# Turning the rows of a second norm by transfers and one VectorE transpose, with the chains around it started three steps sooner

## The chip, the cores and the metric

The kernel runs on one core of a Trainium2 chip. The metric is the device time of one execution in microseconds. Kernels are compared by the median of several executions; the profile is that of one further execution.

## What is computed

Four blocks follow each other on x, which has 8 batch rows of 128 tokens with 512 features. Each block adds a gated update to x, and each reads a layer norm of x:

```
x = x + tanh(g_xattn[0]) * xattn0(layernorm(x), ctx, mask, ...)   # 32 heads of 128
x = x + tanh(g_ffn[0])   * ffn0(layernorm(x), ...)                # 4-bit weights, 512 -> 512
x = x + tanh(g_xattn[1]) * xattn1(layernorm(x), ctx, ...)         # one head of 512
x = x + tanh(g_ffn[1])   * ffn1(layernorm(x), ...)                # dense + routed low-rank update

def xattn1(text, features):
    fn = rmsnorm(features, fn_w)
    Q = rmsnorm(text @ Wq.T + Wq_b, qn_w)
    K = rmsnorm(fn @ Wk.T + Wk_b, kn_w)
    return softmax(Q @ K.T / sqrt(512)) @ fn

def layernorm(x):
    return (x - mean(x)) / sqrt(var(x) + 1e-5)
```

All of it is float32. The kernel gets that accuracy from TensorE by splitting every operand into a high part (type fp32r) and a low part, and by three matmuls for a product: high by high, high by low, low by high.

## The kernel before

The first attention with its weights takes about 765 of the 904 us. What follows is written as chains, one Python generator for a batch row and a block: `ffn0(b)` (L1238), `keys(b)` (L1210, the keys of the second attention), `xattn1(b)` (L1248) and `ffn1(b)` (L1299). `pipeline` (L48) advances all running chains by one step in turn, the newest first. The list `starts` (L1470) says in which step a chain begins. `ffn0(b)` begins in step b + 1 and makes its product psf two steps on; `xattn1(b)` begins in step b + 9; `ffn1(b)` in step b + 17. The weights of `ffn1` are loaded by `ffn1_weights` (L1403), begun in step 13.

TensorE follows the order in which this code issues its instructions (`in_order`, L147). The other engines and the queues follow a planner, which takes what is ready first in a simulated run and, among the ready ones, what the code issued first. `behind(name)` (L140) orders an instruction behind the last one that was marked with that name on the same engine. `mark("x", ...)` stands in `add_to_x` (L793), the VectorE instruction L797 that adds a block's product to x.

The norm is `layernorm` (L1159). In its first step ScalarE writes the row minus its mean to a tile t of 128 tokens by 512 features (L1170). In the second, TensorE turns the four 128 by 128 blocks of t into PSUM (`transposed`, L1143, tile name tph in the trace), ScalarE casts them to the high part and VectorE subtracts for the low part (`parts_of`, L1153, through `split`, L168), tile name h1T, h2T or h3T. Then ScalarE squares the row for its sum (L1177), into a tile that nothing reads ("junkh", in buffers with the tag "raw"), and GpSimd turns the sum into an inverse root (`inverse_root`, L419). The third step makes the product: `dense` in `xattn1` gives psq, and VectorE scales it and adds the bias into q (L1253). In `ffn0` the product is psf; there GpSimd first adds the bias row to x (`add_row`, L1189, ordered behind the last inverse root), and L797 adds the product.

Operands of the products lie in tiles with the tag "page", of which there are 14: two for the transposed keys, two for the query weights, four for the context rows (fn), one for each hT, and four with one more for the weights of `ffn1` (bw, lora). A load into a page waits on its queue until a page comes free.

The first norm of the kernel, ahead of the first attention, turns its rows in another manner. `send` (L457) writes a tile to DRAM and reads it back with 32-row blocks exchanged: one write, and one read for each of four groups of 32 partitions, all issued from the queue of SyncE. `turned` (L470) then transposes every 32 by 32 block by one VectorE instruction (L473). `by_rows` (L449) is the layout in which the rows are written for this.

Of the kernel before, what the change touches and what calls it, by code (L numbers as in the profile page):

```python
# [13 lines left out]
AF = mybir.ActivationFunctionType  # L14
ALU = mybir.AluOpType
AX = mybir.AxisListType

P = 128
NB = 8
D = 512  # L20
NDC = D // P
# [6 lines left out]
Q32 = 32  # L28
NQ = P // Q32
# [37 lines left out]
def kernel(  # L67
# [37 lines left out]
    nc = tc.nc  # L105
# [9 lines left out]
    def slot(shape, tag, name, dtype=F32):  # L115
        return sb.tile(shape, dtype, tag=tag, name=name, bufs=TAGS[tag])
# [6 lines left out]
    def wide_row(tag, name, dtype=F32):  # L123
        return slot([P, D], tag, name, dtype)
# [4 lines left out]
    def wide(t):  # L129

        return t.bitcast(F32)
# [4 lines left out]
    def mark(name, inst):  # L136
        marks[name] = inst.ins

    @contextmanager
    def behind(*names):  # L140
        with ExitStack() as stack:
            for name in names:
                stack.enter_context(tc.issue_after(marks[name]))
            yield
# [238 lines left out]
    for inner in range(2):  # L383
        for half in range(2):
            for dc in range(inner * HK, inner * HK + HK):
                if half == 0 and dc == inner * HK:
                    load_half(0, inner)
                t = wide_row("wo", f"cxraw{half}{dc}")
                queue = nc.scalar if dc == half == 0 else nc.sync
# [5 lines left out]
    lnw = wide_row("pT", "lnw")  # L395
# [40 lines left out]
    def row_stats(j):  # L436
# [9 lines left out]
        nc.gpsimd.tensor_tensor(shift, mean, r12, ALU.mult)  # L446
        nc.gpsimd.tensor_scalar_mul(shift, shift, -1.0)

    def by_rows(t):  # L449

        return t.rearrange("p (n dc k) -> p dc n k", n=NQ, dc=NDC)
# [2 lines left out]

        return t.rearrange("p b (n k) -> p n b k", k=Q32)

    def send(b, name, t, tag):  # L457

        through = dram.tile([P, NQ, NDC * Q32], F32, tag="rows", name=f"rows_{name}_{b}", bufs=6)
        nc.sync.dma_start(out=through, in_=t.rearrange("p (n f) -> p n f", n=NQ))  # L460
        moved = slot([P, NQ, NDC, Q32], tag, f"{name}moved_{b}")
        blocks = through.rearrange("(i q) n f -> n q i f", q=Q32)
        for j in range(NQ):
            move = nc.sync.dma_start(
                out=moved[bass.ts(j, Q32)].rearrange("p i b k -> p i (b k)"), in_=blocks[j]
            )
        mark("sent", move)
        return moved

    def turned(b, name, moved, tag):  # L470

        t = slot([P, NDC, P], tag, f"{name}turned_{b}")
        nc.vector.transpose(by_block(t), moved)  # L473
        return t

    def normed(b):
        xq_b = wide_row("wo", f"xq_{b}")
        nc.scalar.activation(
            xq_b, xs[b], AF.Identity, bias=stats[:, b, 5:6], scale=stats[:, b, 2:3]
        )  # L480
        rows = wide_row("wo", f"xrows_{b}")
        nc.vector.tensor_tensor(
            by_rows(rows), *(t.rearrange("p (dc n k) -> p dc n k", n=NQ, dc=NDC) for t in (xq_b, lnw)), ALU.mult
        )
        return send(b, "x", rows, "s")

    def right_pages(name):
        return {n: page([P, 2, HK, HALF * P], f"{name}{n}") for n in RIGHT.values()}
# [482 lines left out]
    rows = []  # L971
# [171 lines left out]
    def transposed(b, name, src):  # L1143
        tag = "sc" if b % 2 and name in SC_NAMES else "av"
        tp = ptile([P, NDC, P], tag, f"tp{name}_{b}")
        for dc in range(NDC):
            nc.tensor.transpose(tp[:, dc, :], src[:, bass.ts(dc, P)], ident)  # L1147
        return tp

    def work(b, name, tag, shape=(P, D), dtype=F32):  # L1150
        return slot(list(shape), tag, f"{name}_{b}", dtype)

    def parts_of(b, name, src):  # L1153

        t = work(b, name, "page", (P, NDC, 2, P), F32R)
        split(t[:, :, 0, :], t[:, :, 1, :], src)
        return t

    def layernorm(b, name, gate=None):  # L1159


        negm = col(f"nm{name}", b)
        nc.scalar.mul(negm, col(f"sum{name}", b), -1.0 / D)
        t = work(b, name, "wo")
        src, dst = xs[b], t
        if name == "h1":

            dst = t.rearrange("p (jj a r) -> p r a jj", jj=NDC, a=2)
            src = src.rearrange("p (r a jj) -> p r a jj", a=2, jj=NDC)
        nc.scalar.activation(dst, src, AF.Identity, bias=negm)  # L1170
        yield
        tp = transposed(b, name, t)
        if name == "h3" and b > 2:
            turns.pop(b - 3)()
        hT = parts_of(b, f"{name}T", tp)
        ss = col(f"ss{name}", b)
        nc.scalar.activation(  # L1177
            work(b, f"junk{name}", "raw"), xs[b], AF.Square, bias=negm, accum_out=ss
        )
        r = col(f"r{name}", b)  # L1180
        inverse_root(r, ss, 1e-5)
        rg = r
        if gate is not None:
            rg = col(f"rg{name}", b)
            nc.gpsimd.tensor_tensor(rg, r, gate, ALU.mult)
        yield
        return hT, r, rg
# [9 lines left out]
        return ps  # L1197

    def inverse_rms(b, name, src):
        junk = work(b, f"junk{name}", "raw")  # L1200
        ss = col(f"ss{name}", b)
        mark("rms", nc.scalar.activation(junk, src, AF.Square, accum_out=ss))
        r = col(f"ir{name}", b)
        inverse_root(r, ss, 1e-6)
        return r
# [42 lines left out]
    def xattn1(b):  # L1248
        half, j = divmod(b, HALF)
        hT, rh, _ = yield from layernorm(b, "h2")  # L1250
        ps = dense(b, "q", hT, wq1_p)
        q = work(b, "q", "wo")
        nc.vector.scalar_tensor_tensor(q, ps, rh, bq, ALU.mult, ALU.add)  # L1253
        r = inverse_rms(b, "q", q)
        nc.gpsimd.tensor_scalar_mul(r, r, float(D) ** -0.5)
        yield
        tp = transposed(b, "q", q)
        qT = work(b, "qT", "v", (P, NDC, P))
        nc.scalar.copy(qT, tp)
        yield  # L1260
        sc = ptile([P, P], "sc", f"s1_{b}")
        for fc in range(NDC):
            nc.tensor.matmul(
                sc,
                lhsT=qT[:, fc, :],
                rhs=kTs[half][:, fc, j, :],
                start=(fc == 0),
                stop=(fc == NDC - 1),
            )
        p = work(b, "p1", "v", (P, P))  # L1270
        nc.scalar.copy(p, sc)
        nm = col("nm1", b)
        nc.vector.tensor_reduce(nm, p, AX.X, ALU.max, negate=True)
        nc.vector.tensor_tensor(nm, nm, r, ALU.mult)
        yield
        sm = col("sm1", b)
        nc.scalar.activation(p, p, AF.Exp, bias=nm, scale=r, accum_out=sm)
        rs = col("rs1", b)
        nc.vector.reciprocal(rs, sm)
        nc.vector.tensor_tensor(rs, rs, tgx1, ALU.mult)  # L1280
        yield
        tp = ptile([P, P], "av", f"tpp1_{b}")
        nc.tensor.transpose(tp, p, ident)
        pT = work(b, "pT1", "v", (P, 2, P), F32R)

        rc = rcs[:, b : b + 1]
        nc.scalar.activation(pT[:, 0, :], tp, AF.Copy, scale=rc)
        nc.vector.scalar_tensor_tensor(
            pT[:, 1, :], tp, rc, wide(pT[:, 0, :]), ALU.mult, ALU.subtract
        )  # L1290
        yield
        av = ptile([P, D], "mm", f"av1_{b}")
        product(av, [((pT[:, 0, :], pT[:, 1, :]), fns[b])])
        add_to_x(b, av, rs, "h3")
        yield
# [107 lines left out]
    def ffn1_weights():  # L1403
        for dc in range(NDC):
            t = page([P, 2, 2, NS], f"bw{dc}")
            nc.sync.dma_start(out=wide(t).rearrange("p a h n -> p a (h n)"), in_=bw_kept[:, dc])
            for half in range(2):
                bw[dc, half] = [t[:, part, half] for part in range(2)]
        t = page([P, 2, D], "lora")
        nc.sync.dma_start(out=wide(t), in_=lora_kept)  # L1410
        lora.extend(t[:, part] for part in range(2))
        nc.sync.dma_start(out=rb, in_=router_b.partition_broadcast(P))

        em_i = keep([P, NR], "em_i", I32)
        nc.sync.dma_start(out=em_i, in_=expert_map.partition_broadcast(P))
        em_f = keep([P, NR], "em_f")
        nc.vector.tensor_copy(em_f, em_i)
        e_i = slot([P, NE, NR], "moved", "e_i", I32)
        nc.gpsimd.iota(e_i, pattern=[[1, NE], [0, NR]], base=0, channel_multiplier=0)
        nc.vector.tensor_copy(twice, e_i)  # L1420
        nc.vector.tensor_tensor(
            twice, twice, em_f.unsqueeze(1).to_broadcast([P, NE, NR]), ALU.is_equal
        )
        nc.vector.tensor_scalar_mul(twice, twice, 2.0)
        yield
# [43 lines left out]

    starts = [[ending()], ffn[:1], ffn[1:2], ffn[2:3], [ffn[3], key[0]]]  # L1470
    starts += [[ffn[b], key[b - 3]] for b in range(4, NB)]
    starts += [[att[0], key[5]], [att[1], key[6]], [att[2], key[7]]] + [[c] for c in att[3:] + last]
    starts[6].append(query_weights())
    starts[13].append(ffn1_weights())
    with in_order(*ORD):
        pipeline(starts)

# [71 lines left out]
```

## Time and profile before

| | before |
|---|---|
| median of 3 runs | 905.67 us (905.53 to 907.04) |
| the profiled execution's own time | 906.13 us |
| its span, first to last instruction | 904.3 us |
| mean granted clock of TensorE | 0.999 |
| transposes tph, all three norms | 96, median 272 ns long |
| L1170, row minus mean, ScalarE | 24, median 725 ns |
| L170, low part of h2T, VectorE | 8, median 681 ns |
| L169, high part of h2T, ScalarE | 8, median 587 ns |
| L473, VectorE transpose of 128x512 | 8, median 706 ns |
| L1192, row addition on GpSimd | 32 of 128x256, median 740 ns |

The span is what the profile's rows cover; the execution's own time is 1.8 us longer. A row names a line of the kernel, an engine, an operation, the tiles written and read, and a duration. TensorE overlaps neighbouring matmuls, so what one costs is the distance between starts and not its length. In rows of waits, "<-" names what ended the wait.

### The profile page before, as it was taken

How to read it: one execution, taken by the hardware profiler on the slowest of the kernel's cores; microseconds unless marked ns; L12 is line 12 of the kernel's file. 1: busy time of each engine (PE TensorE's matmuls, PEld its weight loads, DVE VectorE, ACT ScalarE, POOL GpSimd, SP SyncE). 2: the span in 40 equal slices, each digit the busy share in tenths (PEclk: the TensorE clock that was granted, in tenths of full speed). 3: DMA queues.
4: the chain of work that ended last, by engine and by line, in shares of the span. 5: the costliest groups of instructions: out<-in, count | busy, mean ns of one | idle time of the engine just before them, and what ended most of it. 6: DMA issues, size and time to landing. Idle time of an engine off the chain costs nothing.

```text
span 904.3 us, 16418 instructions
## 1 busy us (share of the span) xinstructions
PE 897.8 (99%) x5349; PEld 796.7 (88%) x5349; DVE 676.9 (75%) x1361; ACT 502.0 (56%) x1422; POOL 463.1 (51%) x513
## 2 busy tenths in 40 slices
PE   9999999999999999999999999999999999999998
PEld 7887888888888899999999999999999998888897
DVE  7898887778889866777677667766686877565587
ACT  6666565666655555545536345453554544588862
POOL 2455543123323436747748567593766844265441
PEclk9999999999999999999999999999999999999999
DMA  8666568888765957577485765755756566713001
GB/s 285 220 215 224 198 217 296 276 278 302 259 229 203 310 180 209 162 213 219 154 236 154 211 209 159 214 186 184 216 176 205 174 186 181 299 47 143 1 24 71
DMA packets 130982, 179.19 MB, mean 198 GB/s; under 512 B 17744, under 2 KB 59472, under 8 KB 129872
## 3 DMA queue, kind: packets, MB, share of 16 engines
q1 hardware_dynamic: 130752, 177.88, 61.9%
q8 instruction: 42, 0.69, 0.3%
q14 instruction: 44, 0.36, 0.1%
q10 hardware_dynamic: 144, 0.26, 0.1%
HBM read 111.96 MB, written 66.13 MB: 197 GB/s over the span
## 4 chain that ended last, share of the span: by engine, by line
PE 96%; DVE 2%; ACT 1%; DMA 0%; issue 0%; DVEq 0%; ACTq 0%
PE c_v L178 7%; PE c_v L179 6%; PE c_v L182 6%; PE pso L182 6%; PE pso L178 6%; PE pso L179 6%; PE sc L712 6%; PE av L776 6%; PE c_q L178 6%; PE c_q L182 6%; PE c_q L179 6%; PE c_k L178 5%; PE c_k L179 5%; PE c_k L182 5%; PE tph L1147 1%; PE c_k L617 1%
## 5 line engine op out<-in xcount | busy, mean ns | idle before, releaser
L729 ACT ACTIVATE s<-s,nm 128x128 f32<-128x128 f32 x256 | 99.8, 392 | 79.0 <-DVE nm L719 55.8
L797 DVE SCALAR_TENSOR_TENSOR x<-pso,tg,x 128x512 f32<-128x512 f32 x128 | 93.5, 741 | 51.2 <-PE pso L182 50.4
L737 POOL TENSOR_TENSOR s<-s,rs 128x512 f32<-128x512 f32 x64 | 66.7, 1043 | 113.4 <-DVE rs L735 54.8
L178 PE MATMUL pso<-wo_h,a 128*128 128x512 f32 x256 | 101.9, 411 | 0.0
L179 PE MATMUL pso<-wo_l,a 128*128 128x512 f32 x256 | 101.5, 397 | 0.0
L182 PE MATMUL pso<-wo_h,a 128*128 128x512 f32 x256 | 101.0, 395 | 0.1
L178 PE MATMUL c_v<-wvP,cxT 128*128 128x256 f32 x288 | 84.8, 294 | 0.3 <-ACT v L253 0.3
L182 PE MATMUL c_v<-wvP,cxT 128*128 128x256 f32 x288 | 81.4, 283 | 0.0
L179 PE MATMUL c_v<-wvP,cxT 128*128 128x256 f32 x288 | 81.4, 283 | 0.0
L777 ACT CAST a<-av 128x512 fp32r<-128x512 f32 x64 | 37.3, 584 | 75.3 <-PE av L776 74.9
L699 POOL TENSOR_TENSOR s<-mneg,bias 128x512 f32<-128x512 bf16 x64 | 75.5, 1180 | 0.3 <-PE pso L182 0.3
L776 PE MATMUL av<-pT,v 128*128 128x128 f32 x512 | 71.2, 274 | 0.0
L776 PEld LDWEIGHTS av<-pT,v 128*128 128x128 f32 x512 | 67.1, 191 | 2.8
L712 PE MATMUL sc<-k,q 128*128 128x128 f32 x464 | 65.8, 274 | 0.0
L712 PEld LDWEIGHTS sc<-k,q 128*128 128x128 f32 x464 | 61.9, 191 | 3.2
L178 PE MATMUL c_v<-wvP,cxB 128*128 128x256 f32 x216 | 62.1, 289 | 0.0
L778 DVE TENSOR_TENSOR a<-av,a 128x512 fp32r<-128x512 f32 x64 | 43.4, 679 | 24.8 <-ACT a L777 24.5
L179 PE MATMUL c_v<-wvP,cxB 128*128 128x256 f32 x216 | 61.2, 283 | 0.0
L182 PE MATMUL c_v<-wvP,cxB 128*128 128x256 f32 x216 | 61.1, 283 | 0.0
L182 PEld LDWEIGHTS pso<-wo_h,a 128*128 128x128 f32 x256 | 48.2, 188 | 10.8 <-DVE a L778 1.3
L170 POOL TENSOR_TENSOR wo_l<-raw_wo,wo_h 128x512 fp32r<-128x512 f32 x32 | 41.4, 1292 | 31.2 <-ACT wo_h L169 31.2
L715 DVE TENSOR_TENSOR s<-sc,s 128x512 f32<-128x512 f32 x64 | 43.7, 683 | 17.2 <-PE sc L712 12.3
(275 smaller groups left out, 2810.5 us busy)
## 6 DMA issues: line engine op xcount, KB each, us to landing
keys<-keys SPq DMA_DIRECT2D x64, 256.0 KB, 3.3
queries<-queries SPq DMA_DIRECT2D x64, 256.0 KB, 3.1
through<-s SPq DMA_DIRECT2D x64, 256.0 KB, 2.3
moved<-through SPq DMA_DIRECT2D x256, 64.0 KB, 3.0
q<-queries SPq DMA_DIRECT2D x58, 256.0 KB, 3.9
k<-keys SPq DMA_DIRECT2D x58, 256.0 KB, 4.3
raw_wq<-in_wq_dram SPq DMA_DIRECT2D x32, 256.0 KB, 4.0
raw_wv<-in_wv_dram SPq DMA_DIRECT2D x32, 256.0 KB, 4.8
```

What stands on the lines that cost most here:

```text
L170: mark("low", (low_engine or nc.vector).tensor_tensor(low, src, wide(high), ALU.subtract))
L178: nc.tensor.matmul(out, lhsT=lh, rhs=rh, start=first, stop=False, **more)
L179: nc.tensor.matmul(out, lhsT=lh, rhs=rl, start=False, stop=False, **more)
L182: nc.tensor.matmul(out, lhsT=ll, rhs=rh, start=False, stop=last, **more),
L699: nc.gpsimd.tensor_tensor(s, mneg[:, half], bias.unsqueeze(2).to_broadcast([P, NQ, HALF, Q32]), ALU.add)
L712: nc.tensor.matmul(ps[:, j, :], lhsT=q[:, cols], rhs=k[:, cols], start=True, stop=True)
L715: nc.vector.tensor_tensor(s, by_block(ps), s, ALU.add)
L729: e = nc.scalar.activation(one, one, AF.Exp, bias=nm[:, j : j + 1], accum_out=sm[:, j : j + 1])
L737: mark(f"norm{u}", nc.gpsimd.tensor_tensor(s, s, factors, ALU.mult))
L776: nc.tensor.matmul(av[:, b, :], lhsT=v[:, cols], rhs=pT[:, b, :], start=True, stop=True)
L778: mark("al", nc.vector.tensor_tensor(al, av, wide(ah), ALU.subtract))
L797: "x", nc.vector.scalar_tensor_tensor(xs[b], ps, factor, xs[b], ALU.mult, ALU.add, **out)
```

## The change

It touches the second norm (name "h2", in `xattn1`) alone, and the order around it. The centring copy L1170 writes t in the layout of `by_rows`. In the same step t is sent through DRAM, the write issued from ScalarE's queue and the reads from SyncE's. Three steps with nothing in them are added, and `xattn1(b)` begins in step b + 6, so that the turning stays in step b + 10 as before. There one VectorE transpose takes the place of the four on TensorE; it is ordered behind the last instruction marked "x". The split then reads SBUF in place of PSUM. The moved and the turned rows take buffers with the tag "raw", and the squares of all norms write to one tile "junk" with the tag "kq". The query result L1253 is now marked "x" too. `ffn1_weights` begins in step 14, and its loads of bw and lora are ordered behind the last read of `send` ("sent"). In `starts` the chains `keys(5)` to `keys(7)` keep their steps.

```diff
+    def of_rows_by_block(t):
+        return t.rearrange("p (dc n k) -> p dc n k", n=NQ, dc=NDC)
...
-    def send(b, name, t, tag):
+    def send(b, name, t, moved, queue=nc.sync):
 
         through = dram.tile([P, NQ, NDC * Q32], F32, tag="rows", name=f"rows_{name}_{b}", bufs=6)
-        nc.sync.dma_start(out=through, in_=t.rearrange("p (n f) -> p n f", n=NQ))
-        moved = slot([P, NQ, NDC, Q32], tag, f"{name}moved_{b}")
+        queue.dma_start(out=through, in_=t.rearrange("p (n f) -> p n f", n=NQ))
...
+    def blocks_tile(tag, name):
+        return slot([P, NQ, NDC, Q32], tag, name)
...
+    junk = wide_row("kq", "junk")
...
+        far = name == "h2"
+        if far:
+            dst, src = by_rows(t), of_rows_by_block(src)
         nc.scalar.activation(dst, src, AF.Identity, bias=negm)
-        yield
-        tp = transposed(b, name, t)
+        if far:
+            moved = send(b, name, t, blocks_tile("raw", f"{name}moved_{b}"), nc.scalar)
+        yield
+        for _ in range(3 * far):
+            yield
+        if far:
+            with behind("x"):
+                tp = turned(b, name, moved, "raw")
+        else:
+            tp = transposed(b, name, t)
...
         nc.scalar.activation(
-            work(b, f"junk{name}", "raw"), xs[b], AF.Square, bias=negm, accum_out=ss
+            junk, xs[b], AF.Square, bias=negm, accum_out=ss
         )
...
     def inverse_rms(b, name, src):
-        junk = work(b, f"junk{name}", "raw")
...
-        nc.vector.scalar_tensor_tensor(q, ps, rh, bq, ALU.mult, ALU.add)
+        mark("x", nc.vector.scalar_tensor_tensor(q, ps, rh, bq, ALU.mult, ALU.add))
...
             t = page([P, 2, 2, NS], f"bw{dc}")
-            nc.sync.dma_start(out=wide(t).rearrange("p a h n -> p a (h n)"), in_=bw_kept[:, dc])
+            with behind("sent"):
+                nc.sync.dma_start(
+                    out=wide(t).rearrange("p a h n -> p a (h n)"), in_=bw_kept[:, dc]
+                )
...
         t = page([P, 2, D], "lora")
-        nc.sync.dma_start(out=wide(t), in_=lora_kept)
+        with behind("sent"):
+            nc.sync.dma_start(out=wide(t), in_=lora_kept)
...
-    starts += [[att[0], key[5]], [att[1], key[6]], [att[2], key[7]]] + [[c] for c in att[3:] + last]
+    starts += [[key[b]] for b in range(5, NB)] + [[] for _ in range(5)] + [[c] for c in last]
+    for b in range(NB):
+        starts[6 + b].insert(0, att[b])
     starts[6].append(query_weights())
-    starts[13].append(ffn1_weights())
+    starts[14].append(ffn1_weights())
```

More of the change, by code (lines that the diff above doesn't have):

```diff
@@ L481, in normed @@
         rows = wide_row("wo", f"xrows_{b}")
[L482 to L485, printed above, removed]
+        nc.vector.tensor_tensor(by_rows(rows), of_rows_by_block(xq_b), of_rows_by_block(lnw), ALU.mult)
+        return send(b, "x", rows, blocks_tile("s", f"xmoved_{b}"))
     def right_pages(name):
```

## Prediction, made before the changed kernel was run

> **What bounds the kernel now.** I read the busy shares first, then the windows from 787 us on, TensorE's waits there, and last the timelines of TensorE, GpSimd and VectorE around 814 to 821 us, where the change begins to act. Shares and one window:
>
> ```profile
> PE 897.8 (99%) x5349; PEld 796.7 (88%) x5349; DVE 676.9 (75%) x1361; ACT 502.0 (56%) x1422; POOL 463.1 (51%) x513
> ...
> 797.40:820.85 23.45, 23.45 (x126) 19.70 (x125) 16.14 (x38) 18.11 (x48) 21.28 (x45) 1.00 0.28 94
> ```
>
> TensorE sets the end. In the window (columns: length, then busy time of PE, PEld, DVE, ACT, POOL, then clock, DMA share and GB/s) it never pauses, and the one wait found for it after 760 us is 0.3 us. But POOL is at 21.28 of 23.45 us in the same stretch, a share that its 51% over the span hides. TensorE's timeline there (columns: start, length, instruction):
>
> ```profile
> 813.34 0.60 PE L1147 MATMUL tpk<-ident,k 128*128 128x128 f32 x4
> 813.78 0.60 PE L1147 MATMUL tph<-ident,h 128*128 128x128 f32 x4
> 814.14 0.48 PE L178 MATMUL psf<-wf,h1T 128*128 128x512 f32 x1
> 814.45 0.39 PE L179 MATMUL psf<-wf,h1T 128*128 128x512 f32 x1
> 814.68 0.39 PE L182 MATMUL psf<-wf,h1T 128*128 128x512 f32 x1
> ...
> 816.98 0.60 PE L1147 MATMUL tpk<-ident,k 128*128 128x128 f32 x4
> 817.42 0.60 PE L1147 MATMUL tph<-ident,h 128*128 128x128 f32 x4
> 817.77 0.48 PE L178 MATMUL psq<-wq,h2T 128*128 128x512 f32 x1
> ...
> 820.59 0.60 PE L1147 MATMUL tpk<-ident,k 128*128 128x128 f32 x4
> ```
>
> The reader should read starts, not lengths. The tph at 813.78 belongs to the second norm of batch row 0, the one at 817.42 to row 1; the psf block from 814.14 is row 7's first feed-forward product, and psq from 817.77 is row 0's query product. What stands around them on GpSimd and VectorE:
>
> ```profile
> 797.40 0.19 POOL L421 TENSOR_SCALAR cols<-cols 128x1 f32<-128x1 f32 x1 [12.53 <-ACT junkk L1202]
> ...
> 816.90 0.55 POOL L426 TENSOR_TENSOR cols<-cols,neghalf 128x1 f32<-128x1 f32 x1
> 817.42 1.44 POOL L1192 TENSOR_TENSOR x<-x,bias 128x256 f32<-128x256 f32 x2
> ...
> 817.28 0.69 DVE L170 TENSOR_TENSOR h2T<-tph,h2T 128x512 fp32r<-128x512 f32 x1
> 818.89 0.75 DVE L797 SCALAR_TENSOR_TENSOR x<-psf,cols,x 128x512 f32<-128x512 f32 x1 [0.92 <-POOL x L1192]
> ```
>
> Row 7's product is done at 816.98, but its addition to x (L797) waits for GpSimd's row addition and starts at 818.89. Row 0's low part (h2T at 817.28) stands ahead of that addition on VectorE.
>
> **What is removed.** Thirty-two TensorE transposes. Their length (272 ns) is not their price, since they overlap. A block moves the next start by 0.36 us (813.78 to 814.14), and the matmul behind it takes 0.31 us to its follower where the steady step is 0.23: together 0.44 us, the same as from tpk to tph. Eight blocks: 8 x 0.44 = 3.5 us, all on the path, in a stage where TensorE never pauses. The Trainium skill ("VectorE: DVE Perf Modes", The three transpose paths) gives 390 ns for a 128x128 bf16 transpose on TensorE; by that the 32 would be an estimated 12.5 us. The row says a quarter of it.
>
> **What is added.** *VectorE*: eight transposes of 128x512, 0.70 us each by the same operation at L473 and L761, 5.6 us; VectorE is busy 5.1 to 8.7 of every 10 us in 810 to 870, so the time itself hides there. *ScalarE*: the centring copies (0.72 us) move forward, and the eight writes to DRAM are issued from its queue, 0.40 us each by the one such issue in the trace (L390), about 0.47 with the broken overlap between two activations (0.72 long, 0.62 apart): 8 x 0.47 = 3.8 us. In 797 to 821 ScalarE waits 4.4 + 0.8 = 5.2 us, 1.05 to 1.28 us a step before L1163. One copy and one issue (0.62 + 0.47 = 1.1) just fit into such a gap. *SyncE*: 32 reads, 0.43 us to issue; between 800 and 815 us its queue issues nothing and stands before bw, which is moved, and a round trip (2.1 us write, four issues, 2.1 us landing, rows L460 and L464) takes 6 us of the four steps of 3.6 us it is given. The weights that would stand ahead of the reads (bw, lora, at 815.80 and 824.42, waiting on pages) are put behind the last read and one step later; they land in 5.3 us and are first used at 856.0, so that is hidden. If that cover failed, each microsecond late is one on TensorE. The scratch output in one buffer, written by ScalarE alone in order, and the splits that now read SBUF I cost at nothing; a cast is 0.57 us from PSUM and a square of 128x512 from SBUF 0.62, so the bounds are 0 and 0.05 x 8.
>
> **The new wait.** VectorE's transpose of row 0 is ordered behind the last addition marked "x" when it is traced. The order in that step is newest chain first, so it is row 7's feed-forward addition, the one at 818.89. Behind the transpose stand the cast, the low part and, on TensorE, whose order is fixed, psq of row 0. The addition frees VectorE at 819.57; two semaphore instructions 0.1, transpose 0.70, cast 0.57, handing on 0.2: psq starts at about 821.15, and its low part, done at about 821.7, is needed by the third matmul, 0.55 later, just so. TensorE arrives at 817.77 less two removed blocks (0.88) plus tpk, which now comes ahead (0.44): 817.33. It waits 3.8 us. This one wait costs 3.8 against 3.5 saved. Row 1 waits for the same addition but has psq of row 0 before it; rows 2 to 7 are behind the query result two rows back (L1253), with 3.7 us of TensorE work (psq 2.8, two blocks of 0.44) for 2.9 us of chain (0.75 + 0.70 + 0.57 + 0.68 and 0.2 to hand on).
>
> Two smaller terms. GpSimd runs from 797.40 to 820.85 without a wait, and what starts it is the square on ScalarE that follows row 0's centring copy; the new issue stands between them. Bounds 0 and 0.47; I take 0.4, as the copy stands directly before that square already. Key rows on VectorE (two of 0.44 us) or the next transpose (0.70) may go ahead of a low part: 0 to 0.7, I take 0.2, since 0.4 us of slack stands in most steps.
>
> **The clock.** What a pause of 3.8 us does to it no row in mid-span shows. Both ends of the span do:
>
> ```profile
> 903.00:903.50 0.50, 0.00 (x0) 0.00 (x0) 0.00 (x0) 0.00 (x0) 0.00 (x0) 0.86 0.11 33
> 903.50:904.00 0.50, 0.00 (x0) 0.00 (x0) 0.00 (x0) 0.00 (x0) 0.00 (x0) 0.50 0.00 0
> ```
>
> The last matmul ends at 900.78; the granted clock falls to 0.50 at about 903.4, 2.6 us later. At the start, nine matmuls of 128x512 from 5.28 to 9.19 step by 0.43 us instead of 0.23 (the clock column says 1.00 there all the same): 9 x 0.20 = 1.8 us. So the bounds are 0 and 1.8; a pause of 3.8 is nearer to the 2.6 that brought the fall than to the 0.3 that didn't, and I take 1.8. The Trainium skill ("TensorE: Matmul & The Clock Gate", Why this matters for your kernels) warns of pauses over about 3 us, which speaks against this change; its Part 1 has a free-running window of 3.4 us that must be idle. By that window a pause of 3.8 us would fall on a whole one about one time in ten, an estimate, and the sum would lack the 1.8.
>
> **Sum.** -3.5 + 3.8 + 0.4 + 0.2 + 1.8 = +2.7 us. The profiled execution has a span of 904.3 and a time of 906.13, 1.8 around it; it becomes a span of 907.0 and 908.8. It lies 0.46 above the median of 905.67, so the median becomes 908.4 us, slower by 0.3%.
>
> **Rivals.**
> *The clock holds.* The same wait without the fall: +0.9, 906.6. For it: the pause is not much longer than 2.6 us, and parts of it may be cut. Against: the row at the end of the span.
> *The gain stays (the other side).* Row 0's addition is not late: if GpSimd's row additions came 2 us sooner, the wait shrinks to 1.8 us or, with the transpose outside that order, to none, -3.5 to -1.7, and no clock falls. 902.2 at best, 902.7 with the small terms. For it: ScalarE loses a copy a step from 820 us on, and TensorE's work is less by a sure 3.5 us. Against: GpSimd's 21.28 of 23.45 us, and nothing taken off it. It decides from 1.7 us of wait downwards.
> *Rows that come late.* Seven "raw" buffers hold five moved rows and two turned ones, so rows 6 and 7 are read only once a turned row is split, and the bw pages queue behind these reads. Also ScalarE: 3.8 + 5 x 0.62 = 6.9 us more in 797 to 821 against 5.2 us of waits, so the GpSimd chain may slip by up to 1.7 in place of the 0.4: +4.0; with one row late by 0.5 besides, +4.5: 910.2. Against: four steps of slack.
>
> **How the numbers follow.** Clock falls 45%, clock holds 21%, gain stays 21%, late rows 13%. The measurement tells nothing under 0.2%, 1.8 us. The forecast's own range is 907.3 to 909.6; the whole takes in the gain and the late rows, 902.3 to 910.2. Faster: 0.21. Same: the clock-holds case and a little of the forecast, 0.25. Slower: the rest, 0.54.
>
> **What would show it.** In the changed profile: no tph between psf and psq; a TensorE pause of 3 to 4 us before the first psq, released by ScalarE's h2T; a transpose on VectorE just behind L797 of row 7; psq steps of 0.43 us for some 4 us after it, with a granted clock below 1.00; GpSimd unbroken from about 797.8. I am wrong if the first transpose stands ahead of that addition, if L797 of row 7 starts before 817.5, or if TensorE waits in several places for the moved rows.

## The result, and the profile after

| | before | after |
|---|---|---|
| median | 905.77 us (905.53 to 907.04, 6 runs) | 909.27 us (907.84 to 909.73, 6 runs) |
| profiled execution, its span | 906.13 us, 904.3 us | 909.14 us, 907.4 us |
| mean granted clock | 0.999 | 0.998 |

The changed kernel is slower: a ratio of 1.0036, with a 95% interval of 1.0026 to 1.0046. TensorE's busy time and all that it waited for from 760 us on, first from the page and then from the view of waits (columns: us in total, times, the longest):

```profile
PE 897.0 (99%) x5317; PEld 792.7 (87%) x5317; DVE 680.4 (75%) x1369; ACT 503.3 (55%) x1422; POOL 461.4 (51%) x513
```

```profile
PE psq L182 <- DVE h2T L170: 1.9, 4, 1.2
PE psq L178 <- ACT h2T L169: 1.5, 1, 1.5
PE c_v L178 <- ACT v L253: 0.3, 1, 0.3
```

The 32 matmuls are gone (5349 to 5317), and in a stage where TensorE had one wait of 0.3 us stand two new groups, 3.4 us together. TensorE's timeline shows where the longest are:

```profile
816.34 1.04 PE L1151 MATMUL tpk<-ident,k 128*128 128x128 f32 x8
818.86 0.50 PE L178 MATMUL psq<-wq,h2T 128*128 128x512 f32 x1 [1.48 <-ACT h2T L169]
819.19 0.39 PE L179 MATMUL psq<-wq,h2T 128*128 128x512 f32 x1
820.77 0.50 PE L182 MATMUL psq<-wq,h2T 128*128 128x512 f32 x1 [1.19 <-DVE h2T L170]
...
821.95 0.63 PE L178 MATMUL psq<-wq,h2T 128*128 128x512 f32 x1
822.38 0.63 PE L179 MATMUL psq<-wq,h2T 128*128 128x512 f32 x1
```

Row 0's query product waits twice, for its high part (1.48) and for its low part (1.19). From the product's sixth matmul on, at 821.57, the next starts come 0.38 to 0.43 us apart in place of 0.23. The window over it shows a lower granted clock (third from the end; in windows of 1 us it reads 0.50 from 822 to 825):

```profile
820.00:830.00 10.00, 9.05 (x38) 7.13 (x39) 5.79 (x10) 6.12 (x13) 2.48 (x7) 0.83 0.45 122
```

VectorE's timeline gives what the two parts stood behind:

```profile
816.77 0.75 DVE L801 SCALAR_TENSOR_TENSOR x<-psf,cols,x 128x512 f32<-128x512 f32 x1 [0.72 <-POOL x L1209]
...
817.45 0.71 DVE L479 STREAM_TRANSPOSE h2turned<-h2moved 128x512 f32<-128x512 f32 x1
818.08 0.84 DVE L1232 SCALAR_TENSOR_TENSOR k<-v,rcs,bk 128x256 f32<-128x256 f32 x2
818.83 1.28 DVE L1247 TENSOR_TENSOR kT<-tpk,qkn 128x512 f32<-128x512 f32 x2
820.03 0.68 DVE L170 TENSOR_TENSOR h2T<-h2turned,h2T 128x512 fp32r<-128x512 f32 x1
```

L801 is L797 of before: row 7's addition, and the transpose of row 0 stands right behind it. Then come two pairs of instructions on the keys ("x2"), and only then row 0's low part at 820.03.

To compare one stage between kernels without what happened ahead of it, the tables below also give its length: from the c_v matmul of the first attention that waits 0.3 us for ScalarE (at 777.39 before) to the first matmul of the last block, o<-bw (at 856.02). It is 78.63 us before and 81.88 after. So +3.25 us are made in this stage, against +3.1 in the span; what comes behind it costs nothing more.

Within it the starts of TensorE's instructions add up as follows. The pause in front of the first psq is 1.72 us over the plain step of the transposes, the one in front of its third matmul 1.35. The slow steps behind them cost 1.6: seven matmuls together 1.33 above 0.23 each, and a block of transposes 0.25. Waits and late steps at rows 2 to 5 are 1.6. With the 3.5 removed that is 1.72 + 1.35 + 1.6 + 1.6 - 3.5 = +2.8; the other 0.5 lies in differences under 0.12 a step.

### The profile page after: what moved, and what is told of

It reads as the page before. It is cut to its first block, busy times and chain, and to the rows that moved or that the text cites. A ratio compares the mean times of both kernels' runs of the same rounds, so it can differ in the third digit from the quotient of the medians.

```text
span 907.4 us, 16429 instructions
## 1 busy us (share of the span) xinstructions
PE 897.0 (99%) x5317; PEld 792.7 (87%) x5317; DVE 680.4 (75%) x1369; ACT 503.3 (55%) x1422; POOL 461.4 (51%) x513
## 4 chain that ended last, share of the span: by engine, by line
PE 93%; ACT 2%; DMA 2%; DVE 1%; issue 1%; SPq 0%; DVEq 0%; ACTq 0%
PE c_v L178 7%; PE c_v L179 6%; PE c_v L182 6%; PE pso L182 6%; PE pso L178 6%; PE pso L179 6%; PE sc L716 6%; PE av L780 6%; PE c_q L178 6%; PE c_q L179 6%; PE c_q L182 6%; PE c_k L178 5%; PE c_k L179 5%; PE c_k L182 5%; PE psq L182 1%; PE o L178 1%
## 5 line engine op out<-in xcount | busy, mean ns | idle before, releaser
L801 DVE SCALAR_TENSOR_TENSOR x<-pso,tg,x 128x512 f32<-128x512 f32 x128 | 93.5, 742 | 51.5 <-PE pso L182 50.7
```

What stands on the lines that cost most here:

```text
L801: "x", nc.vector.scalar_tensor_tensor(xs[b], ps, factor, xs[b], ALU.mult, ALU.add, **out)
```

## Experiments

Three accounts were set against each other first: the order behind "x" makes the wait; the fall of the clock makes the loss; something else that the change brought makes it (copies, loads, the order of the steps). The letters in an expectation are explained there; A and B do not mean the same in all of them. The runs shared their runs of the kernel before: 905.82 us (25 runs) for e1 to e4, 906.07 (24) for e5 to e9, 905.87 (26) for e10 to e12. Stage lengths and waits are from one profiled execution each.

| run | median us (runs) | ratio to before, 95% | stage us |
|---|---|---|---|
| after | 909.27 (6) | 1.0036, 1.0026 to 1.0046 | 81.88 |
| e1_row01_free | 908.33 (8) | 1.0027, 1.0017 to 1.0037 | 81.59 |
| e2_steps_only | 907.75 (11) | 1.0019, 1.0010 to 1.0028 | 80.93 |
| e3_fill | 909.37 (6) | 1.0034, 1.0022 to 1.0046 | 80.96 |
| e4_pages | 907.67 (11) | 1.0019, 1.0010 to 1.0028 | 79.47 |
| e5_row0_sooner | 908.42 (5) | 1.0033, 1.0020 to 1.0046 | 80.66 |
| e7_steps_sooner | 905.83 (11) | 1.0001, 0.9992 to 1.0010 | 78.67 |
| e8_rows01_sooner | 905.98 (11) | 1.0003, 0.9994 to 1.0012 | 78.29 |
| e9_all_sooner | 903.30 (8) | 0.9975, 0.9964 to 0.9985 | 76.74 |
| e10_sooner_pages_as_after | 904.33 (10) | 0.9982, 0.9973 to 0.9991 | 76.93 |
| e11_before_pages | 906.11 (11) | 1.0003, 0.9994 to 1.0012 | 78.61 |
| e12_sooner_on_pe | 906.10 (11) | 1.0000, 0.9991 to 1.0008 | 78.92 |

**The order behind "x" taken from rows 0 and 1.**

```diff
-            with behind("x"):
+            with behind(*("x",) * (b > 1)):
                 tp = turned(b, name, moved, "raw")
```

> The changed kernel, but the VectorE transposes of rows 0 and 1 are no longer ordered behind the last addition marked x (rows 2 to 7 still are). Theory A (the order behind row 7's late addition makes the pause before the first query product, and the pause drops the clock): TensorE's 1.48 us wait for the high part of row 0 shrinks below 0.4 us, the wait for its low part may stay (up to 1.6 us, since that part still stands behind row 7's addition, key rows and key blocks on VectorE), no matmul steps by 0.43 us, and the time falls from 909.3 to between 906.2 and 907.6 us. Theory B (the moved rows come late, or VectorE is short of time): the wait stays where it is and the time stays at 909.3 within 0.7.

908.33: 0.9 us below the changed kernel, with intervals that overlap, and between the ranges of the two theories. The executions at a clock of 1.000 took 907.51 to 908.31, the one of the changed kernel 907.84. VectorE's timeline of this run:

```profile
815.98 0.70 DVE L479 STREAM_TRANSPOSE h2turned<-h2moved 128x512 f32<-128x512 f32 x1
816.79 0.75 DVE L801 SCALAR_TENSOR_TENSOR x<-psf,cols,x 128x512 f32<-128x512 f32 x1
...
817.46 0.88 DVE L1232 SCALAR_TENSOR_TENSOR k<-v,rcs,bk 128x256 f32<-128x256 f32 x2
818.26 0.68 DVE L1247 TENSOR_TENSOR kT<-tpk,qkn 128x512 f32<-128x512 f32 x1
818.86 0.68 DVE L170 TENSOR_TENSOR h2T<-h2turned,h2T 128x512 fp32r<-128x512 f32 x1
```

The transpose now precedes row 7's addition, but the low part still stands behind that addition and the keys, and the cast on ScalarE starts at 817.03, behind a square of 0.72 us that starts at 816.31. TensorE waits 0.85 and 1.14 us at row 0 and 0.76 at row 2. One instruction was set free; the rest of row 0's chain was not.

**The steps alone.** The chains begin three steps sooner as in the change, and the marks, the scratch tile and the later loads stay, but TensorE turns the rows and nothing is sent:

```diff
-            dst, src = by_rows(t), of_rows_by_block(src)
-            moved = send(b, name, t, blocks_tile("raw", f"{name}moved_{b}"), nc.scalar)
...
-        if far:
-            with behind("x"):
-                tp = turned(b, name, moved, "raw")
-        else:
-            tp = transposed(b, name, t)
+        tp = transposed(b, name, t)
```

> The changed kernel with its steps, its one scratch tile, its marks and its later weight loads, but the second norm's rows are turned by four TensorE transposes again and nothing is sent through DRAM. Theory A (what costs is the VectorE transpose in its place, with all that stands before it): no TensorE pause over 0.4 us after 800 us, and 905.8 us within 0.8, as before the change. Theory C (moving the centring copies and the weight loads costs by itself): 907.5 us or more.

907.75: 1.9 us slower than before, though nothing is turned by VectorE and nothing is sent. TensorE's timeline of this run:

```profile
816.34 0.60 PE L1151 MATMUL tph<-ident,h 128*128 128x128 f32 x4
816.77 0.60 PE L1151 MATMUL tpk<-ident,k 128*128 128x128 f32 x4
817.21 0.60 PE L1151 MATMUL tph<-ident,h 128*128 128x128 f32 x4
818.38 0.50 PE L178 MATMUL psq<-wq,h2T 128*128 128x512 f32 x1 [0.57 <-ACT h2T L169]
...
820.26 0.50 PE L182 MATMUL psq<-wq,h2T 128*128 128x512 f32 x1 [1.15 <-DVE h2T L170]
```

Before, row 0's tph stood at 813.78, ahead of row 7's first feed-forward product, and had 4 us until psq. Here row 0's tph (816.34) stands behind that product, just ahead of psq. The turning stayed in step 10, but a step lets the newest chain go first. `xattn1(0)`, begun in step 9, was newer than `ffn0(7)` of step 8; begun in step 6 it is older. So in the same step row 0 is turned, cast and split behind row 7's feed-forward work. The time is the one theory C gave, but this cause, the order within the step, is one that no expectation had named. TensorE's clock is not part of it: all eleven executions read 0.999 or 1.000.

**TensorE kept at work.** Six matmuls on the identity ahead of row 0's product; the work is added, nothing is left out:

```diff
+        if b == 0:
+            idle = ptile([P, P], "av", "filling")
+            for _ in range(6):
+                nc.tensor.matmul(idle, lhsT=ident, rhs=ident, start=True, stop=True)
```

> The changed kernel with six further 128x128 matmuls of the identity (12 instructions, some 1.3 us at the full clock, result unread) on TensorE just ahead of row 0's query product, where TensorE stands still for 1.48 us. Theory A (the fall of the clock is a price of its own, about 1.6 us): the matmuls fill the pause, the clock stays at 1.00, no step of 0.43 us, and the time falls to 907.7 within 0.6. Rival D (the slow steps are not due to the pause): the steps of 0.43 us stay and the time stays at 909.3, or rises by what doesn't fit into the pause.

909.37, no gain. Of the wait of 1.48 us for the high part 0.39 is left, but the wait for the low part (1.18) stays, and one of 0.80 appears at row 2. The profiled execution has no 0.43 us steps and a stage of 80.96, yet it took 910.52, the longest of the six: it came to this stage 2.3 us later than the changed kernel did (779.46 against 777.17), and nothing here shows why. Four of the six executions have a mean clock of 0.997 or 0.998, as five of the changed kernel's have. This doesn't separate the clock from the wait, and what the clock costs stays undecided by it.

**The last block's weights two steps later.**

```diff
-    starts[14].append(ffn1_weights())
+    starts[16].append(ffn1_weights())
```

> The changed kernel with the loads of the last weights begun in step 16 in place of 14, so that they take pages two steps later. Theory E (rows 4 and 5 wait for their low part because a cast must wait for the page of the row before, held by the last product): ScalarE's casts of h2T no longer wait for psq in rows 3 to 5, the waits of 0.18 to 0.30 us at L182 go, and the time falls by 0.5 to 1.0 to about 908.5. Rival F (VectorE's order, with the next row's transpose ahead of the low part, makes these waits): no change, 909.3 within 0.5.

907.67, lower than expected. Row 0 still waits; TensorE's timeline of this run:

```profile
818.96 0.50 PE L178 MATMUL psq<-wq,h2T 128*128 128x512 f32 x1 [1.74 <-ACT h2T L169]
...
820.87 0.50 PE L182 MATMUL psq<-wq,h2T 128*128 128x512 f32 x1 [1.19 <-DVE h2T L170]
```

The waits at rows 4 and 5 (0.30 and 0.21) are gone. In the changed kernel ScalarE's casts of these rows wait 1.00 and 1.58 us for the product of the row before; here they don't, so pages held by those loads had made them late. The eleven executions fall into groups by clock: four at 1.000 took 906.20 to 906.75, five at 0.998 took 907.18 to 908.86, two at 0.996 took 908.78 and 909.11. In the same way the one execution of the changed kernel at 1.000 took 907.84, the five others 909.10 to 909.73. So the clock falls in some executions of one kernel and not in others: the traced one (906.71) has the two waits above and a clock of 1.00 behind them. Where it falls 1.1 us (medians 906.67 and 907.76) to 2.3 us (908.95) go along with it. The fall is a part of the loss and not all of it: at a clock of 1.000 e1 took 907.51 to 908.31, and e4 a median of 906.67, against 905.82 before.

**Row 0 turned one step sooner.** The place in the step order (theory G) was then tried by itself: row 0 is turned in step 9, ahead of row 7's feed-forward product, and waits a step before its product. First in the changed kernel, then in the run of the steps alone:

```diff
-        for _ in range(3 * far):
+        for _ in range((3 - (b == 0)) * far):
             yield
...
-        yield
+        for _ in range(1 + (far and b == 0)):
+            yield
         return hT, r, rg
```

> The changed kernel, but row 0 alone is turned and split one step sooner (in step 9, ahead of row 7's feed-forward product in the order of the code, where the kernel before had it) and then waits a step; every other row as it was. Theory G (starting the second attention's chains three steps sooner makes them older than row 7's feed-forward chain, so row 0 is turned behind that chain's product and addition, and this place makes the two waits of 1.48 and 1.19 us and the fall of the clock): both waits of row 0 go, the clock stays at 1.000, and the time is 909.3 - 2.7 - 1.6 = 905.0, up to 0.9 more if row 1 now waits: 904.7 to 906.0. Theory A2 (it is the VectorE transpose, whatever its place): 908 or more.

> The kernel e2_steps_only (four TensorE transposes, nothing sent, chains three steps sooner) with row 0 turned one step sooner in the same way. Theory G: the two waits of 0.57 and 1.15 us that e2_steps_only showed at row 0 go, and with them its whole loss: 905.9 within 0.6. Theory C (moving the centring copies and the weight loads costs): it stays at 907.7 within 0.6.

Without the VectorE transposes (e7) the whole loss of the steps alone is gone: 905.83, a stage of 78.67 against 78.63, and no wait. With them (e5) it is 908.42 and far from what theory G gave; it lies in the range of A2, by which the VectorE transpose costs whatever its place, and which e9 below excludes. The wait went one row on; TensorE's timeline of e5 at row 1:

```profile
820.08 0.60 PE L1151 MATMUL tpk<-ident,k 128*128 128x128 f32 x4
821.78 0.50 PE L178 MATMUL psq<-wq,h2T 128*128 128x512 f32 x1 [1.10 <-ACT h2T L169]
...
822.96 0.52 PE L182 MATMUL psq<-wq,h2T 128*128 128x512 f32 x1 [0.45 <-DVE h2T L170]
823.29 0.61 PE L178 MATMUL psq<-wq,h2T 128*128 128x512 f32 x1
823.70 0.63 PE L179 MATMUL psq<-wq,h2T 128*128 128x512 f32 x1
```

Row 0 goes through without a wait, row 1 now waits 1.10 and 0.45, and the slow clock follows it. Row 1's transpose stood at 820.37 on VectorE, behind row 7's addition (817.71) and four instructions on the keys.

**Rows 0 and 1, then all rows.** Both with the weights in step 16. The diff is that for all rows (e9); for two rows (e8) `far` in the two new lines holds for b < 2 alone, as b == 0 above.

```diff
-        for _ in range(3 * far):
+        for _ in range(2 * far):
             yield
...
-        yield
+        for _ in range(1 + far):
+            yield
         return hT, r, rg
...
-    starts[14].append(ffn1_weights())
+    starts[16].append(ffn1_weights())
```

> The changed kernel with rows 0 and 1 turned one step sooner, and the last weights' loads begun in step 16. If theories G and E hold together, all pauses over 0.5 us go and about 0.5 us of small ones stay: 905.8 - 3.5 + 0.5 to 1.5 = 902.8 to 904.0, faster than the kernel before by 0.2 to 0.3%. If the VectorE transposes push other work on VectorE out in its place, new waits of psq show and the time is 905 or more.

> As e8_rows01_sooner, with every row turned one step sooner, so that each split has a whole step of cover and takes its page a step earlier. If late low parts alone remain in e8_rows01_sooner, they go here: 902.3 to 903.3. If pages run short because each row holds one for two steps, casts wait for psq and it is slower than e8_rows01_sooner by 0.5 or more.

With two rows the same wait comes at row 2; TensorE's timeline of e8:

```profile
826.02 0.50 PE L178 MATMUL psq<-wq,h2T 128*128 128x512 f32 x1 [1.21 <-ACT h2T L169]
```

905.98 misses the expected gain by 2 and is the other case that was named, a new wait of psq. Rows 0, 1 and 2 were late in turn (the changed kernel, e5, e8): whichever is the first row not moved waits, and it does so only where VectorE turns the rows, since e7 with row 0 moved had no wait. With all rows it is 903.30, faster than before by 0.25% (0.15 to 0.36), at the upper edge of what was expected, though the wait that went was for a high part and not for low parts alone. The waits of this run in the view from 766 us on:

```profile
PE tpk L1151 <- ACT k L1245: 0.8, 2, 0.6
...
PE psq L182 <- DVE h2T L170: 0.2, 1, 0.2
```

And row 0 on VectorE:

```profile
814.74 0.70 DVE L479 STREAM_TRANSPOSE h2turned<-h2moved 128x512 f32<-128x512 f32 x1
...
816.33 0.68 DVE L170 TENSOR_TENSOR h2T<-h2turned,h2T 128x512 fp32r<-128x512 f32 x1
817.64 0.75 DVE L801 SCALAR_TENSOR_TENSOR x<-psf,cols,x 128x512 f32<-128x512 f32 x1 [0.63 <-POOL x L1210]
```

The transpose and the low part are now both done ahead of row 7's addition, which is no sooner than in the changed kernel (817.64 against 816.77, behind GpSimd). The order behind "x" is still there; it means an older addition.

**What the gain is made of.** Three last runs: e9 with the weights back in step 14 (e10), the kernel before with its weights in step 16 in place of 13 (e11), and e9 with its rows turned by TensorE, with the edit of the steps alone (e12).

> All rows are turned one step sooner, as in the run at 903.3 us, but the weights of the last block begin in step 14 again, as in the changed kernel. Theory H (the place of the rows in the step order is what cost the gain; the weights' loads matter little once no row is waited for): 902.9 to 904.3 us, no wait of TensorE for h2T over 0.4 us. Theory P (the later loads carry a good part of that run's gain, as the run with them alone was 1.6 us under the changed kernel): 904.7 to 905.9 us, with low-part waits of 0.2 to 0.3 us at rows 4 and 5.

> The kernel before with nothing but its loads of the last block's weights begun in step 16 in place of step 13. Theory H: TensorE never waited for anything there, so within 0.5 us of the kernel before, 905.4 to 906.5 us. Theory P: the later loads help whatever stands ahead of them, 903.5 to 905.0 us; the gain of the 903.3 us run would then not be one of the transposes.

> The kernel of 903.3 us, all rows one step sooner and the weights in step 16, but with the rows turned by TensorE and nothing sent. What is left between the two is the 32 transposes, priced at 3.5 us, less the waits of about 0.9 us that the 903.3 us run still has. Theory H: 905.4 to 906.4 us, 2.1 to 3.1 us above it. The rival (the order of the steps and the loads made the gain, and the transposes are hidden): 903.0 to 904.4 us.

e10 took 904.33, 0.03 above theory H's range; its interval overlaps e9's, and its stage is 76.93 against 76.74: the later loads are worth 0.2 us in the stage; a wait of 0.20 at row 4 is back. This run differs from the changed kernel in nothing but the place of the turning: 904.33 against 909.27, a ratio of 0.9982 against 1.0036. e11 took 906.11, the same as before. e12 took 906.10 with a stage of 78.92. Between e12 and e9 only the way of turning differs: 2.2 us in the stage. As e9 still waits 0.60, 0.19 and 0.17 us where e12 waits for nothing, the transposes alone are worth an estimated 2.18 + 0.96 = 3.1 us there, if each wait is paid in full.

## Why the prediction was right, and where its terms were off

The forecast was slower by 2.7 us, at 908.4, by a wait in front of row 0's query product that eats the gain, and by a clock that falls behind it. The direction held, and 909.27 lies inside the forecast's own range and the whole. Four signs of the mechanism are in the trace: no tph before psq, the VectorE transpose right behind row 7's addition, TensorE stopped in front of the first psq and released by ScalarE's h2T, 0.43 us steps later with a granted clock of 0.83 over 10 us. Two are not: the pause is 1.48 us and not 3 to 4, and GpSimd starts at 796.21 and twice waits in between (0.48 and 0.24). Of the three conditions named as showing the prediction wrong two are met: row 7's addition starts before 817.5, and TensorE waits at several rows (0, 2, 4 and 5). The sum term by term:

- *Removed, -3.5.* e9 against e12 gives about 3.1, near to it. By the 390 ns for a bf16 block of the Trainium skill ("VectorE: DVE Perf Modes", The three transpose paths) it would have been an estimated 12.5; the runs show a quarter of it.
- *The wait, +3.8, was mis-sized: 3.1 (1.72 + 1.35).* It assumed row 7's addition at 818.89 as before. It came at 816.77, since GpSimd's chain started at 796.21 in place of 797.40 and the row addition of row 7 went ahead of an inverse root that it had stood behind. GpSimd's timeline:

```profile
796.21 0.19 POOL L421 TENSOR_SCALAR cols<-cols 128x1 f32<-128x1 f32 x1 [11.57 <-ACT junk L1218]
...
815.04 1.70 POOL L1209 TENSOR_TENSOR x<-x,bias 128x256 f32<-128x256 f32 x2
816.82 0.46 POOL L421 TENSOR_SCALAR cols<-cols 128x1 f32<-128x1 f32 x2
```

  That undid 2.1 us of lateness and left 1.72 in front of the first psq. But the low part, priced as "just so", gave 1.35 back: it stood behind 1.95 us of work on the keys (818.08 to 820.03).
- *GpSimd's slip, +0.4: none.* The DMA issues on ScalarE took 0.33 us each (one 0.36) and GpSimd started sooner, not later.
- *Late low parts, +0.2: 1.6 at rows 2 to 5*, three waits of 0.18 to 0.30 us with what follows them. A part was pages held for the last block's weights, which e4 shows, and which the prediction had called hidden.
- *The clock, +1.8: 1.6*, in the execution shown; it doesn't fall in every one. The size is right by luck: it was priced for one pause of 3.8 us, longer than the 2.6 read at the end of the span, and no pause came near that.

Mis-sized terms of both signs nearly cancelled, so that the sum came near is luck. What the prediction had too narrow is the cause. It put the whole wait on the order behind "x". e1 took that order away from rows 0 and 1 and won 0.9 us, with intervals that overlap; e2 left out the VectorE transposes and still lost 1.9; e7 got these back by the place alone. The step that missed is that the turning "stays in step b + 10 as before": the step is the same, but within it row 0 falls behind row 7's feed-forward work, on all engines at once. The rival in which the gain stays therefore asked for the wrong thing, a GpSimd 2 us sooner. That came true in the changed kernel (2.1 us), its first pause shrank to 1.72, near the 1.8 us that the rival named, and the gain was lost all the same, to the low part and the clock. In e9 GpSimd's row addition is no sooner, and the gain stays because the turning moved ahead of it: 2.3 us in the ratio (0.25% of 906.07), 1.9 in the stage. The rival of the late rows played no part: in the changed kernel no VectorE transpose of the second norm waited for a transfer.

Why five executions of six lose the clock, and what decides it, stays open.

## What to carry to other kernels

When a chain is begun earlier so that its transfers are hidden, look not only at the step in which its next work lands but at what stands ahead of it in that step on every engine: here the place alone cost 1.9 us (e2), before any cost of the new instructions. Work moved from a saturated engine to a shared one needs more lead there, for every row and not for the first alone: with the fix at one or two rows the wait only went to the next. Keeping the operations and changing their place (e2 and e7), and keeping the place and changing the operations (e12), is what told the two apart.

## What the runs showed of the hardware that was not expected

The granted clock fell behind short pauses. In the changed kernel TensorE's two long waits took 1.48 and 1.19 us, with two matmuls between them; in e5 the fall came behind a wait of 1.10 and one of 0.45. But it did not always come: the traced execution of e4 waited 1.74 and 1.19 us and read 1.00 behind them, the steps alone waited 0.57 and 1.15 us and e8 1.21, and both kept 0.999 or 1.000 in all eleven executions.

The prediction had read 2.6 us from the last matmul to the fall at the end of the span. That is not a fixed time: over the thirteen profiled executions it lies between 1.5 us (e9, last matmul at 897.88) and 3.3 us (e12, at 900.75).

The Trainium skill ("TensorE: Matmul & The Clock Gate", Why this matters for your kernels) warns of gaps over about 3 us; here the granted clock fell without one. Its Part 1 has a free-running window, which would go with a fall that comes and goes between executions of one kernel, as in e4. It also has the fall come after an idle window of about 3.4 us; here matmuls ran between the two pauses, and at the end of the span 1.5 us were enough. No run here tells what share of idle time decides.
